# A two-layer adaLN program of eight batches: a weave with lags, the last batch in one weave, and the token shift's mix by scaled weights

## The chip, the cores and the metric

The kernel runs on one core of a Trainium2 chip. The core has five engines, each with its own instruction queue that is worked off in order: TensorE (PE, with its weight loads shown apart as PEld), VectorE (DVE), ScalarE (ACT), GpSimd (POOL) and SyncE (SP), which here only issues DMAs. The metric is the device time of one execution in microseconds. The kernel before takes 2069.03 us, the median of 3 runs (2065.26 to 2073.69).

## The reference

The input is x, 8 batches of 512 tokens of 128 channels. Two layers follow each other, and each has two halves of the form x + g * F(LN(x) * (1 + c) + s), with s, c and g from a modulation per batch.

```
h = LN(x)*(1+ca)+sa;  x = x + ga * L0_attn(h)        # layer 0, first half
h = LN(x)*(1+cb)+sb;  x = x + gb * L0_ffn(h)         # layer 0, second half
h = LN(x)*(1+ca)+sa;  x = x + ga * L1_attn(h)        # layer 1, first half
h = LN(x)*(1+cb)+sb;  x = x + gb * L1_ffn(h)         # layer 1, second half
```

- L0_attn: LN, then causal attention with 16 heads of 8 channels, and beside it a state-space branch (a causal convolution, a scan over time with 16 states for each of 256 channels, a gate, a product). The two are mixed, and an LN with a GELU FFN (512 hidden) follows.
- L0_ffn: a shared SiLU FFN and 8 experts of the same form, weighted by a router's top 2.
- L1_attn: attention over a band, with batch and sequence changed over, so that for each of 512 positions the 8 batches attend to each other.
- L1_ffn: a token shift. With x' the token before, xr = mu_r*x + (1-mu_r)*x' and xk = mu_k*x + (1-mu_k)*x'; the output is sigmoid(xr W_r) * (relu(xk W_k)^2 W_v).

## The kernel before, in words

**Tiling.** Activations lie channels by tokens, 128 x 512, one tile for a batch; all products are float32 apart from the causal mask, which is added by bfloat16 products with an identity. PSUM has eight banks: a ring of three (`mm_tile`, L148) for all products that leave at once, four for two score tiles of two banks each (`products`, L480), and one for the attention's sum.

**The parts of a batch's work**, all Python generators that issue a few instructions and then yield a cost:
- `head` (L816): load x, two layer norms. `normalised` (L237) is the norm: product with a centring matrix (`_m`), square and copy on ACT, a mean by small products (`_v`), + eps on DVE, the power -1/2 on POOL, a spread by four products (`_rb`), a product on DVE; `layernorm` adds ACT's scale and bias.
- `ssm_inputs` (L655): convolution, gate and steps, and `ssm_scan` (L741): for 16 units of two states, DVE's product hs (L783), two scans (L788), POOL's product of hs (L792), and `add`, a DVE sum of the two states (L764) and a POOL sum into xc (L765). B and C come from DRAM by broadcast loads (bc). `add` of a unit is issued behind the first scan of the next.
- `attention` (L438): four head groups g. `projections` (q, k), `maxima` (s, and DVE's maxima, L520), `shifts` (transposed maxima mT, and DVE's sum into qT, L539), `exponentials` (e, and ACT's exp, L558), `values` (av), `projected` (den, DVE's reciprocal rd, rb, DVE's product, and for each second group the product ao).
- `tail` (L826): LN and GELU FFN of L0_attn, the LN of L0_ffn, and `routing`: r, lg, top 2. `experts` (L934): for the shared FFN and 8 experts four products e (L945) with ACT's SiLU, four products e (L960), and DVE's weighting wb (L968) with a POOL sum moe (L971). `dispatch` writes the weights through DRAM: wT, a store wd, broadcast loads wb.
- `attention2` (L302): LN (lnc), products kv and q, then `attended`: POOL products pr (L358), DVE sums sc (L348), softmax, POOL products pv (L393), DVE sums ao (L387). Its result goes to DRAM (`kept`), apart from the last batch's.
- `mixing` (L1109): for one of eight slices of 448 tokens: load, transpose (aoT), residual xa, LN (lnd), `mixed_channels` (L1060): ACT scales the past token by 1-mu, DVE adds mu times the token (L1067), once for r and once for k; products ck, cr, cv; output transposed (oT) and stored. `closing` and `closed` do the remaining 512 + 512 tokens.

**The order.** PE, ACT and DVE run in the order in which these generators are advanced. `weave` (L200) takes parts with a cost in all and a begin and end, and always advances the part with the least progress. `paced` (L221) adds an order on DVE behind the latest marked softmax instruction. The loop L1004 runs a weave for each batch b: rest of attention(b), scan(b), head(b+1), attention2(b-2), ssm_inputs(b+1), the begin of attention(b+1), and `behind`, which is tail and experts of b-1. After the loop, the score banks are given back (L1025) for a ring of five (`l1_tile`), and a weave lays tail and experts of batch 7 beside attention2(6) and the mixing of slices 0 to 3; another lays attention2(7) beside slices 4 to 7 (L1232); closing follows.

Of the kernel before, what the change touches and what calls it, by code (L numbers as in the profile page):

```python
# [68 lines left out]
MSK, NMSK = _cols(_MASK)  # L69


@with_exitstack
def kernel(
# [126 lines left out]
    def weave(*parts):  # L200

        live = []
        for k, (pieces, whole, begin, end) in enumerate(parts):
            live.append([begin, k, iter(pieces), (end - begin) / whole])
        while live:
            part = min(live)
            cost = next(part[2], None)
            if cost is None:  # L210
                live.remove(part)
            else:
                part[0] += cost * part[3]
# [23 lines left out]
    def normalised(src, name, lane, cost=0.9, n=T, ring=mm_tile, wait=0.0):  # L237
# [5 lines left out]
        yield 0.2  # L243
# [4 lines left out]
        yield 2 * cost - 0.2  # L248
# [16 lines left out]
        yield cost + wait  # L265
# [11 lines left out]
        yield cost  # L277
        return d

    def layernorm(dst, src, scale, bias, name, lane, cost=0.9, n=T, ring=mm_tile, wait=0.0):  # L280
# [3 lines left out]
        yield cost  # L284
# [17 lines left out]
    def attention2(s, at):  # L302
# [6 lines left out]
        for i0 in range(0, NB, 2):  # L309
# [15 lines left out]
            yield 0.9  # L325
# [13 lines left out]
        yield 0.9  # L339
        yield from paced(attended(s, at, q, kv))  # L340

    def attended(s, at, q, kv):
# [13 lines left out]
        for i in range(NQ):  # L356
# [7 lines left out]
            yield 1.6  # L364
# [8 lines left out]
        yield 1.6  # L373
# [16 lines left out]
        for i in range(NQ):  # L390
# [10 lines left out]
            yield 1.6  # L401
# [20 lines left out]
    with ExitStack() as l0:  # L422
# [15 lines left out]
        def attention(b):  # L438
# [23 lines left out]
            def projections(g):  # L462
# [15 lines left out]
                yield 0.9  # L478
# [29 lines left out]
            def maxima(g, step):  # L508
# [19 lines left out]
                yield 0.6 + 0.25 * c0 / P  # L528

            def shifts(g):  # L530
# [10 lines left out]
                yield 1.2  # L541
# [3 lines left out]
            def exponentials(g, step):  # L545
# [15 lines left out]
                yield 0.6 + 0.25 * c0 / P  # L561
# [23 lines left out]
            def projected(g):  # L585
# [14 lines left out]
                yield 0.9  # L600
# [11 lines left out]
                yield 0.9  # L612
# [20 lines left out]

            yield from projections(0)
            for k in range(len(STEPS)):
                yield from maxima(0, k)
            for g in range(NG):
# [3 lines left out]
                )  # L641
                for k in range(len(STEPS)):
                    yield from exponentials(g, k)
                    next(others, None)
                    if g + 1 < NG and k:
                        alone(maxima(g + 1, k - 1))
                    values(g, k)
                    yield 0.85 + 0.25 * k
                    next(others, None)
                if g + 1 < NG:  # L650
                    yield from maxima(g + 1, len(STEPS) - 1)
                alone(others)
            yield from projected(NG - 1)

        def ssm_inputs(b, xn):  # L655
# [36 lines left out]
            yield 1.8  # L692
# [11 lines left out]
            yield 1.7  # L704
# [6 lines left out]
            for c in range(NDI):  # L711
# [15 lines left out]
                yield 0.9  # L727
# [5 lines left out]
                yield 0.9  # L733
            yield 0.9
# [6 lines left out]
        def ssm_scan(b, h, xc, zs, bc, dt, dtx):  # L741
# [27 lines left out]
            for u, (n0, c) in enumerate(units):  # L769
# [16 lines left out]
                yield 0.3  # L786
                for n in range(NN):
# [5 lines left out]
                    yield 0.3  # L793
                    if n == 0 and summed:
                        add(*summed.pop())
                        yield 0.15
                summed.append((n0, c, hs))
            add(*summed.pop())
            yield 0.15
            for c in range(NDI):  # L800
                nc.gpsimd.tensor_mul(xc[c], xc[c], zs[c])
                yield 0.5
            yield 0.5
# [9 lines left out]
            nc.vector.scalar_tensor_tensor(h, ps, beta, h, op0=ALU.mult, op1=ALU.add)  # L813
            yield 1.0

        def head(b):  # L816

            load_x(b)
            yield 0.5
# [6 lines left out]
        def tail(b, h):  # L826
# [5 lines left out]
            for m in range(NFF):  # L832
# [4 lines left out]
                t = wk.tile([P, T], F32, tag="hid", name=f"hid{b}_{m}", bufs=4)  # L837
                nc.scalar.activation(t, ps, AF.Gelu, bias=cv("ffn_b1", m))
                hid.append(t)
            yield 3.4  # L840
# [13 lines left out]
            yield 3.4  # L854
            hm = act.tile([P, T], F32, tag="hm", name=f"hm{b}")
# [5 lines left out]
        def routing(b, hm):  # L861
# [5 lines left out]
            yield 0.9  # L867
# [25 lines left out]
            yield 0.9  # L893
            yield 0.9
# [14 lines left out]
            for _ in range(4):  # L909
                yield 0.9  # L910
# [23 lines left out]
        def experts(b, hm, we):  # L934
            acc = wk.tile([P, T], F32, tag="moe", name=f"moe{b}", bufs=1)
            wd = None
            for e in range(NE + 1):
# [13 lines left out]
                yield 3.4  # L951
# [22 lines left out]
                yield 3.4  # L974
# [4 lines left out]
        ready, inputs, routed = {}, {}, {}  # L979
        nc.sync.dma_start(out=wb_sb, in_=wb)  # L980

        def finish(b, h):

            yield from tail(b, h)
            yield from experts(b, *routed.pop(b))

# [15 lines left out]
        with tc.manual_schedule(engines={mybir.EngineType.PE, mybir.EngineType.Activation, mybir.EngineType.DVE}):  # L1002
            behind = None
            for b in range(NB):  # L1004
# [3 lines left out]
                parts = [(ahead, 42.7, 0.0, 1.0)]  # L1008
                parts.append((paced(ssm_scan(b, h, *inputs.pop(b))), 19.3, 0.0, 0.83))
                if b + 1 < NB:  # L1010
                    parts.append((head(b + 1), 9.5, 0.1, 0.55))
                if b >= 2:
                    parts.append((attention2(b - 2, a2), 23.4, 0.0, 1.0))
                if b + 1 < NB:
                    parts.append((after(b + 1), 8.0, 0.8, 0.97))
                    ahead = attention(b + 1)
                    parts.append((some(ahead, BEGUN), 7.3, 0.85, 1.0))
                if behind:
                    parts.append((behind, 91.5, 0.0, 1.0))
# [5 lines left out]
            banks.close()  # L1025
            pl1 = l0.enter_context(tc.tile_pool(name="pl1", bufs=5, space=PSUM))

            def l1_tile(name):
                return pl1.tile([P, 512], F32, tag="mm", name=name)

            LAST = NB - 1
# [5 lines left out]
            def kept2(name):  # L1037

                t = wk.tile([P, 2, T], F32, tag="ex", name=name)
                return t.rearrange("p k t -> p (k t)").rearrange("p (i k u) -> p i k u", k=2, u=U)  # L1040

            now, past = kept2("now"), kept2("past")
            x7, x0 = (
                act.tile([P, T], F32, tag=f"xc{k}", name=f"xz{k}").rearrange(
                    "p (i u) -> p i u", u=U
                )
                for k in range(2)
            )
            nc.vector.memset(past[:, :, 1, 0:1], 0.0)
            gate = own[:, 10 + NG + NDI * DS :]  # L1050
            nc.vector.tensor_scalar(gate, mods[1][:, 5, :], 0.5, None, ALU.mult)
# [8 lines left out]
            def mixed_channels(name, n, cur, prev, t, r):  # L1060

                for k, mu in enumerate(("mu_r", "mu_k")):
# [315 lines left out]
```

## Time and profile before

The profiled execution took 2073.63 us; its span, from the first to the last instruction, is 2071.8 us with a mean granted TensorE clock of 0.87.

| engine | busy us | share | instructions |
|---|---|---|---|
| PE | 1653.0 | 80% | 8762 |
| PEld | 795.4 | 38% | 8762 |
| DVE | 1441.0 | 70% | 1648 |
| ACT | 985.2 | 48% | 1413 |
| POOL | 1045.2 | 50% | 539 |

| row | count | busy us | mean ns |
|---|---|---|---|
| DVE scan, L788 | 256 | 442.8 | 1732 |
| POOL product, L792 | 128 | 386.7 | 3021 |
| PE first product of the experts, L945 | 576 | 315.5 | 679 |
| DVE product before the scans, L783 | 128 | 249.5 | 1949 |
| POOL sum, L765 | 112 | 199.1 | 1778 |
| DVE maxima, L520 | 256 | 193.9 | 808 |

A float32 product stands in the trace as two matmuls. A row's idle time is that of its engine just before it, and the name behind the arrow is what ended most of it. A wait names the instruction that waited, the one that released it, the time in all, the number and the longest.

### The profile page before, as it was taken

To read this page: it belongs to the slowest core of one execution; us is meant where nothing else is said; L and a number is where in the kernel's file an instruction comes from. 1 tells how busy PE (TensorE), PEld (TensorE's weight loads), DVE (VectorE), ACT (ScalarE), POOL (GpSimd) and SP (SyncE) were. 2 spreads that over 40 slices of the span, in tenths; PEclk is the share of its full clock that TensorE was granted. 3 is DMA by queue.
4 is the path that set the end of the run, shared out by engine and by line. 5 is a ranking of instruction groups with operands and counts; after the bars stand their busy time and mean duration, and the time that the engine had idled before them with its cause. 6 is when DMAs were issued, how large, how long until landed. Compare 5 with 4: busy or idle time off the path is not lost. (4 is left out here: it accounts for less than half of the span.)

```text
span 2071.8 us, 22824 instructions
## 1 busy us (share of the span) xinstructions
PE 1653.0 (80%) x8762; PEld 795.4 (38%) x8762; DVE 1441.0 (70%) x1648; ACT 985.2 (48%) x1413; POOL 1045.2 (50%) x539
## 2 busy tenths in 40 slices
PE   5765888888798887888789788888788768868864
PEld 3332343434343443334334443334333333344442
DVE  1798688647894798668885889568876889352255
ACT  2532555464544644455445554464536454423432
POOL 1566355535673566444772667355763567331131
PEclk9766789998999988999889898999889989968975
DMA  3220123121222122121212122121312122102200
GB/s 101 78 71 21 53 70 99 52 83 56 82 71 78 46 77 82 46 79 59 94 56 83 54 73 78 47 82 60 98 47 78 57 87 81 50 9 76 71 8 18
DMA packets 67405, 135.32 MB, mean 65 GB/s; under 512 B 7864, under 2 KB 23360, under 8 KB 67168
## 3 DMA queue, kind: packets, MB, share of 16 engines
q1 hardware_dynamic: 66816, 131.51, 20.5%
q10 hardware_dynamic: 288, 1.93, 0.3%
q8 instruction: 69, 1.13, 0.2%
q0 software_dynamic: 192, 0.42, 0.1%
q14 instruction: 40, 0.33, 0.1%
HBM read 129.24 MB, written 4.59 MB: 65 GB/s over the span
## 5 line engine op out<-in xcount | busy, mean ns | idle before, releaser
L788 DVE TENSOR_TENSOR_SCAN hs<-da,hs 128x512 f32<-128x512 f32 x256 | 442.8, 1732 | 6.5 <-DVE hs L783 0.5
L792 POOL TENSOR_TENSOR hs<-hs,bc 128x1024 f32<-128x1024 f32 x128 | 386.7, 3021 | 102.2 <-DVE hs L788 83.9
L945 PE MATMUL e<-hm,we 128*128 128x512 f32 x576 | 315.5, 679 | 84.7 <-DVE wb L968 45.6
L558 ACT ACTIVATE ex<-e 128x768 f32<-128x768 f32 (+1 forms) x192 | 158.8, 879 | 317.4 <-PE e L496 317.0
L765 POOL TENSOR_TENSOR xc<-xc,hs 128x512 f32<-128x512 f32 x112 | 199.1, 1778 | 200.1 <-DVE hs L764 200.1
L960 PE MATMUL e<-eh,we 128*128 128x512 f32 x576 | 272.1, 616 | 0.3
L783 DVE TENSOR_TENSOR hs<-bc,dtw 128x1024 f32<-128x1024 f32 x128 | 249.5, 1949 | 0.0
L949 ACT ACTIVATE eh<-e,vec_sb 128x512 f32<-128x512 f32 x288 | 188.5, 686 | 122.1 <-PE e L945 115.2
L520 DVE TENSOR_REDUCE mpad<-s 128x2 f32<-128x256 f32 (+3 forms) x256 | 193.9, 808 | 39.4 <-PE s L496 39.4
L971 POOL TENSOR_TENSOR moe<-moe,wb 128x512 f32<-128x512 f32 x64 | 94.2, 1472 | 223.8 <-DVE wb L968 223.8
L945 PEld LDWEIGHTS e<-hm,we 128*128 128x128 f32 x576 | 111.6, 214 | 241.2 <-issue 89.3
L488 PE MATMUL e<-qT,kT 32*128 32x512 f32 (+3 forms) x1024 | 135.0, 580 | 81.7 <-DVE qT L539 75.3
L750 ACT ACTIVATE da<-dtu,own 128x512 f32<-128x512 f32 x256 | 169.8, 719 | 12.6 <-POOL dtu L737 12.2
L960 PEld LDWEIGHTS e<-eh,we 128*128 128x128 f32 x576 | 108.5, 198 | 127.3 <-issue 113.8
L968 DVE SCALAR_TENSOR_TENSOR wb<-e,vec_sb,wb 128x512 f32<-128x512 f32 x64 | 47.7, 745 | 150.5 <-DMA wb<-wd 58.4
L488 PE MATMUL s<-kT,qT 32*128 32x128 f32 (+3 forms) x1024 | 134.7, 524 | 10.4 <-DVE mpad L520 5.5
L764 DVE TENSOR_TENSOR hs<-hs 128x512 f32<-128x512 f32 x112 | 93.7, 837 | 37.9 <-POOL hs L792 37.9
L393 POOL TENSOR_TENSOR pv<-kv,sc 128x1024 f32<-128x1024 f32 x32 | 62.2, 1952 | 108.4 <-DVE ao L387 90.6
L496 PEld LDWEIGHTS <-ident_b 128*128 128x128 bf16 x1024 | 63.4, 103 | 138.0 <-issue 131.3
L358 POOL TENSOR_TENSOR pr<-kv,q 128x1024 f32<-128x1024 f32 x32 | 88.5, 2777 | 33.6 <-DVE sc L348 18.6
L488 PEld LDWEIGHTS e<-qT,kT 32*128 32x128 f32 x1024 | 51.2, 214 | 139.3 <-DVE qT L539 84.7
L572 PE MATMUL av<-ex,va 128*32 128x512 f32 (+3 forms) x1024 | 99.1, 478 | 0.0
(277 smaller groups left out, 2488.5 us busy)
## 6 DMA issues: line engine op xcount, KB each, us to landing
bc<-bc SPq DMA_DIRECT2D x128, 512.0 KB, 3.8
we<-in_w_dram SPq DMA_DIRECT2D x144, 256.0 KB, 3.1
wb<-wd SPq DMA_DIRECT2D x64, 256.0 KB, 3.3
xin<-in_x_dram SPq DMA_DIRECT2D x8, 256.0 KB, 2.9
wa_sb<-in_wa_dram ACTq DMA_DIRECT2D x1, 1832.0 KB
kept<-ao SPq DMA_DIRECT2D x14, 128.0 KB, 2.5
ai<-kept SPq DMA_DIRECT2D x56, 32.0 KB, 2.2
out_dram<-xout SPq DMA_DIRECT2D x16, 96.0 KB, 2.3
```

The costliest lines, as they stand in the source:

```text
L488: nc.tensor.matmul(tiles[i // 2][:, i % 2, c0 : c0 + n], lhsT=lhs[quadrant(i)], rhs=rhs[quadrant(i)], start=True, stop=False,)
L520: nc.vector.tensor_reduce(mpad[:, qi, 2 * pr : 2 * pr + 2, HD : HD + 1], tiles[pr][:, :, a : a + n], AX.X, ALU.max, negate=True,)
L558: nc.scalar.activation(t[:, :, :c0], tiles[pr][:, :, :c0], AF.Exp)
L572: nc.tensor.matmul(avs[g][quadrant(i), kj * P :], lhsT=va[:, kj, at : at + 32], rhs=ex[i // 2][:, i % 2, c0 : c0 + n], start=(kj == 0), st ...
L750: nc.scalar.activation(da[:, n, :], dt[c], AF.Exp, scale=A_sb[:, c, n0 + n : n0 + n + 1])
L765: nc.gpsimd.tensor_add(y, y, hs[:, 0, :])
L783: nc.vector.tensor_mul(hs, bcs[0], dtx[c].unsqueeze(1).to_broadcast([P, NN, T]))
L788: nc.vector.tensor_tensor_scan(hs[:, n, :], da[:, n, :], hs[:, n, :], 0.0, ALU.mult, ALU.add)
L792: nc.gpsimd.tensor_mul(hs, hs, bcs[1])
L945: nc.tensor.matmul(ps, lhsT=we1[:, m * P : (m + 1) * P], rhs=hm, start=True, stop=True)
L949: nc.scalar.activation(t, ps, AF.Silu, bias=cv("b1", e * NFF + m))
L960: nc.tensor.matmul(ps, lhsT=we2[:, m, :], rhs=hid[m], start=(m == 0), stop=(m == NFF - 1),)
```

## The change

**The weave.** A step may carry, beside its cost, a lag and the PE time that it stands for. `weave` counts the PE time issued so far (`now`). A part whose last step's results are due later than `now` is held back by 0.06 of progress for each unit that is missing. Nearly all steps get a lag and a PE time; those of the scan and of ACT's or DVE's own steps have a PE time of 0. The attention's products for the next group, which were issued without a yield of their own, are now steps too, and its whole cost is 64.3 where it was 42.7. In the scan, `add` is issued behind the second scan of the next unit.

```diff
+class Step(float):
+    def __new__(cls, cost, lag=0.0, pe=None):
+        self = super().__new__(cls, cost)
+        self.lag, self.pe = lag, cost if pe is None else pe
+        return self
+SOON = 0.06
...
-            live.append([begin, k, iter(pieces), (end - begin) / whole])
+            live.append([begin, k, iter(pieces), (end - begin) / whole, 0.0])
+        now = 0.0
         while live:
-            part = min(live)
+            part = min(live, key=lambda p: (p[0] + SOON * max(0.0, p[4] - now), p[1]))
             cost = next(part[2], None)
             if cost is None:
                 live.remove(part)
-            else:
-                part[0] += cost * part[3]
+                continue
+            part[0] += cost * part[3]
+            now += getattr(cost, "pe", cost)
+            part[4] = now + getattr(cost, "lag", 0.0)
...
-        yield cost + wait
+        yield Step(cost + wait, 5.0, 0.9)
...
-                yield 1.2
+                yield Step(1.2, 3.0, 0.5)
...
-                yield 0.3
+                yield Step(0.3, 0.0, 0.0)
                 for n in range(NN):
...
-                    yield 0.3
-                    if n == 0 and summed:
+                    yield Step(0.3, 0.0, 0.0)
+                    if n == NN - 1 and summed:
                         add(*summed.pop())
-                        yield 0.15
+                        yield Step(0.15, 0.0, 0.0)
```

**The last batch.** The loop runs over batches 0 to 6. One weave then holds attention, scan and attention2(5) of the last stage, the tail and experts of batch 6 and of batch 7, attention2(6) and the first four slices. `finish` waits, by steps of no PE time, until the attention and the scan of its batch have been issued whole, and its experts until those of the batch before have. `l1_tile` gives the score banks back at its first use. The last batch's hidden tiles and hm lie in other buffers, and each slice is a part of its own, whose norm buffers are passed on through `lanes`.

```diff
         def finish(b, h):
+            while b not in joined or joined[b] < 2:
+                yield Step(0.3, 1.0, 0.0)
             yield from tail(b, h)
+            while b and not done[b - 1]:
+                yield Step(0.3, 1.0, 0.0)
             yield from experts(b, *routed.pop(b))
+            done[b] = True
...
             weave(
-                (behind, 91.5, 0.0, 1.0),
-                (
-                    chain(through(LAST - 1), *(pair(i, (MIX, SECOND)) for i in range(0, SHARE, 2))),
-                    23.4 + 11.7 * SHARE, 0.0, 1.0,
+                (ahead, 64.3, 0.0, 0.86),
+                (paced(ssm_scan(LAST, h, *inputs.pop(LAST))), 19.3, 0.0, 0.74),
+                (attention2(LAST - 2, a2), 23.4, 0.03, 0.8),
+                (behind, 92.0, 0.0, 1.0),
+                (finish(LAST, h), 92.0, 0.87, 1.85),
+                (through(LAST - 1), 23.4, 1.02, 1.3),
+                *(
+                    (mixing(i, (MIX, SECOND)[i % 2]), 11.0, 1.33 + 0.13 * i, 1.6 + 0.13 * i)
+                    for i in range(SHARE)
                 ),
             )
```

**The mix.** Behind attention2(6), `begun` scales the weights W_r and W_k by mu and by 1-mu, four tiles of 128 x 128 on ACT. `mixed_channels` then adds two products in PSUM, of the token and of the past token, in place of the scaling on ACT and the sum on DVE.

```diff
+                kept2["w"] = act.tile([P, 4, C], F32, tag="at", name="wmix", bufs=3)
+                for k, name in enumerate(("r", "k")):
+                    for j, mu in enumerate((cv(f"mu_{name}"), omu[:, k : k + 1])):
+                        nc.scalar.activation(
+                            kept2["w"][:, 2 * k + j, :], cwb(name), AF.Identity, scale=mu
+                        )
...
-                for k, mu in enumerate(("mu_r", "mu_k")):
...
-                    nc.scalar.activation(tk, prev, AF.Identity, scale=omu[:, k : k + 1])
-                    nc.vector.scalar_tensor_tensor(
-                        tk, cur, cv(mu), tk, op0=ALU.mult, op1=ALU.add
-                    )
-                yield 0.9
+                def product(k, ps):
+                    for j, rhs in enumerate((cur, prev)):
+                        nc.tensor.matmul(
+                            ps, lhsT=kept2["w"][:, 2 * k + j, :], rhs=rhs,
+                            start=(j == 0), stop=(j == 1),
+                        )
```

## The prediction

> **What bounds the kernel now.** I read the page's busy shares first (PE 80%, DVE 70%, ACT 48%, POOL 50% of 2071.8 us), then cut the span into stages at the moments when TensorE transposes a batch's first score maxima (mT, group 0), then asked one steady stage for its waits. From 452.7 us on five stages last 228.0 to 228.9 us each, so one of them stands for all. Columns of the next fence: stretch, its length, busy time of PE, PEld, DVE, ACT, POOL, the granted clock, DMA share, GB/s.
>
> ```profile
> 63.40:240.20 176.80, 125.37 (x804) 60.69 (x805) 142.09 (x130) 60.91 (x90) 94.65 (x45) 0.71 0.16 50
> ...
> 909.20:1137.80 228.60, 192.96 (x1057) 90.40 (x1056) 172.34 (x192) 118.85 (x165) 128.78 (x66) 0.90 0.23 70
> ...
> 1595.20:1807.30 212.10, 165.78 (x941) 75.53 (x939) 159.47 (x168) 103.62 (x141) 124.03 (x59) 0.92 0.22 67
> 1807.30:1964.80 157.50, 126.59 (x400) 66.43 (x400) 57.98 (x101) 56.18 (x102) 33.82 (x23) 0.84 0.19 54
> 1964.80:2071.80 107.00, 59.76 (x233) 37.61 (x232) 57.91 (x76) 29.79 (x63) 25.22 (x15) 0.68 0.05 13
> ```
>
> PE has 193 us of work in a stage of 228.6 and idles 35. Where, the stage's waits say (time in all, times, longest):
>
> ```profile
> PE e L488 <- DVE qT L539: 9.6, 2, 6.9
> PE e L945 <- DVE wb L968: 6.1, 1, 6.1
> PE lna_rb L269 <- POOL lna_r L264: 4.6, 1, 4.6
> PE ln_rb L269 <- POOL ln_r L264: 4.1, 1, 4.1
> PE e L945 <- ACT eh L949: 3.9, 4, 2.1
> PE lnc_m L242 <- DVE xT L975: 3.4, 1, 3.4
> PE rb L604 <- DVE rd L599: 2.0, 1, 2.0
> ```
>
> Seven waits make 33.7 of the 35 us, and nearly all end with DVE, or with a POOL power that DVE feeds. But DVE is not a slow bystander: by the rows' durations it has 145 us of work from a stage's first mT to the end of its scan, where PE has 147. **In that stretch the two engines are equally loaded**, both queues are in order, and PE can run only a few tiles ahead (three banks in the shared ring). After it PE has 50 us with little for DVE.
>
> **Part 1, the order.** I take the order in which the changed program's instructions stand and give each the mean duration of its row. For each wait: PE work between producer and consumer, before and after. lnc_m behind xT: 2.5, then 6.7 us, so the 3.4 us go. e of group 2 behind its mT: 0, then 4.2, so 2.7 go. rb behind den of group 1: 2.6, then 10.5, so 2.0 go. e of group 3 waits 6.9 because qT's sum stands behind a DVE sum that waits 4.7 us for POOL's product; the change issues that sum one scan later, so I let 6.9 go. wb's 6.1 us is a round trip through DRAM behind one of the scan's loads in SP's queue; from wT to wb's place on DVE stood 6.9 us, now 10.3, so 6.1 go too. That is 21 us. lna_rb: 3.7, then 6.2. ln_rb (the L0 FFN's norm): 0, then 5.0. If those two also went, 30 us a stage would go.
>
> They do not, because of **what the order puts ahead of these instructions on DVE**. A scan piece now carries no PE time and no lag, so while the other parts are held back by their penalties, scan pieces are taken one after another. Stretches of DVE work that are scan alone: the longest was 9.5 us, now 13.0 and 12.0 in a steady stage; in the last batch 19.6, 14.6, 12.0 and 11.8 where it was 9.5. Walked through for a steady stage, with DVE's qT sum at 0:
> - ln_r stood 5.8 us after it, now 13.5; its power takes 1.6 and stands behind two products of 3.0 and one of 1.8 on POOL. PE reaches ln_rb 10.4 us on: it waits about 6 where lnc_m and ln_rb waited 7.5.
> - lna_rb waits about 3.5 (4.6).
> - lnb_d stands behind the run of 12.0 and starts near 66.7. Behind it are ACT's hm and PE's router product r, which PE reaches near 59: a new wait of 8, and 3 more for the next bank of the ring.
> - The second half has DVE 131 us on where PE is 118 on (wb of expert 4): about 6.5.
> - The eh waits of 3.9 stay.
>
> Sum 31 us where 34 were: 3 gained. A bound without any wait says the same from the other side: DVE's work up to the worst place plus PE's work behind it was 58 + 146 = 204 us, now 58 + 154 = 212.
>
> **The rule that speaks against longer scan runs.** The rows (min/median/max ns):
>
> ```profile
> L788 DVE TENSOR_TENSOR_SCAN hs<-da,hs x256: 1192/1218/3256, 76.4 to 1755.9; 128x512 f32<-128x512 f32 x128
> L783 DVE TENSOR_TENSOR hs<-bc,dtw x128: 1192/2218/3061, 74.7 to 1750.1; 128x1024 f32<-128x1024 f32 x128
> L792 POOL TENSOR_TENSOR hs<-hs,bc x128: 2336/3319/3351, 78.8 to 1759.5; 128x1024 f32<-128x1024 f32 x128
> ```
>
> The same instruction takes 1.2 or 3.2 us. The Trainium skill, "SBUF — State Buffer", section "Who interferes with whom", says that a DVE instruction with two SBUF inputs and a GpSimd instruction that reads SBUF exclude each other, whole instruction by whole instruction, while a DVE instruction with one SBUF input is free. By the rows' means a unit of two states costs DVE 1.95 + 2 x 1.73 + 0.84 = 6.25 us. By the rule, in a run with no other DVE work to lie beside POOL, it costs its own 1.2 + 2 x 1.2 + 0.67 = 4.3 plus POOL's 2.34 + 1.26 = 3.6: 7.9, a quarter more. The runs over 7 us hold 23 us more than before: by the row 0, by the rule up to 6 us a stage; I take 3, since half of each run meets a POOL product already now. New waits that I cannot place (the power behind POOL products, ACT's hm ahead of qT and kT in its queue): bounds 0 and 6.6 (two products of 3.3), I take 3. A steady stage then costs -3 + 3 + 3 = +3; stages 1 to 6: **+18** (bounds -60 and +48).
>
> Stage 0 (no experts; DVE 142 of 177): the bound goes from 118 + 34 = 152 to 106 + 54 = 160 us. I take **+6** (0 to +10).
>
> **Part 2, the last batch in one weave.** `finish` waits until attention and scan have both joined. In the order the last batch's FFN norm stands right behind its last attention product, as before, and 5 us of PE work before the end of batch 6's experts, where it stood 2 behind them (batches count from 0): **hardly anything is overlapped anew.** What does change is the scan: it is to be done by 0.74. Bound before: DVE 142 to the last mT, then PE 42: 184 (taken: 212). Now DVE 123 to expert 2 of batch 6, then PE 82: 205, because PE reaches so with 112 us done where it had 139. Of the +21 some falls into waits that were there; **+12** (0 to +25).
>
> The last batch's FFN and experts (157.5 us, PE work 130 in both orders): the mixing tiles come 25 us of PE work later, so the fetch wait (5.0), an eh wait behind the softmax (5.8) and one ck wait (2.9) go: **-12** with 1.7 kept back (-15 to 0).
>
> **Part 3, the mix by products.** It removes the 16 DVE sums of 1045 ns and 16 ACT scalings of 607, and those of the two closing tiles; PE gets a second ck and cr each: 8 x (1.22 + 1.03) + 2 x (1.45 + 1.09) = 23.1 us, by the rows of the first ones. Four small ACT scalings make the weights behind batch 6's second attention, in no one's way.
>
> ```profile
> L1067 DVE SCALAR_TENSOR_TENSOR mix<-xa,vec_sb,mix 128x384 f32<-128x384 f32 x16 | 16.0, 1045 | 10.0 <-ACT mix L1066 10.0
> ...
> L1072 PE MATMUL ck<-mix,wb_sb 128*128 128x384 f32 x16 | 10.5, 750 | 16.1 <-DVE mix L1067 16.1
> ```
>
> In the end stretch (107 us, PE 60) the waits of ck (13.3), ck_z (5.2), lnc_m (3.1) go, and half of an lnd_rb wait (6.3) that stood behind the mix. But PE's work behind the experts grows from 55 to 77 us by the order: 8 us of it stand before lnc_m and 9 more before the queries, so the last attention, a chain of POOL and DVE, starts that much later. +22 + 8 for that start's own exposed share - 25 = **+5** (-10 to +20).
>
> **Sum.** The profiled execution took 2073.63 us, 1.8 more than its span: 2073.6 + 18 + 6 + 12 - 12 + 5 = 2102.6. The three timed runs have their median 4.6 us below the profiled one, so I predict **2098 us**.
>
> **Rivals.**
> - *The scan runs decide* (the sum above), 0.48; own range 2080 to 2125.
> - *The lags win* (faster), 0.28. For it: the distances grow at all seven waits, and DVE has 56 us idle a stage to absorb the runs. It decides where ln_rb and r wait under 3 us each instead of 6 and 8: then a steady stage gains 6, six of them 36, and with +4, +8, -12, +5 the time is 2073.6 - 31 - 4.6 = 2038.
> - *A wash*, 0.12: waits change places at equal size, near 2070. The equal load of the two engines speaks for it.
> - *The port decides*, 0.12: every unit costs near 7.9 in the runs and DVE bounds each stage at +8 to +10: 56 + 10 + 20 + 0 over 2069 is 2155.
>
> What can be told from no change here is about 0.5%. Faster by more 0.28, within 0.12, slower 0.60. The range, 2030 to 2140, takes in the first three and the lower part of the last.
>
> **What would show it.** Right: steady stages near 232 us; a new PE wait at r behind hm or lnb_d of some 8 us; no lnc_m wait; scans with a mean above 1.73 us; the last batch's so with PE 112 us in; ck without a wait. Wrong: stages under 225 us, or ln_rb's wait under 3 us, which would mean that the penalties hide more than the runs cost.

## The result, and the profile after

The changed kernel takes 2247.61 us (median of 4 runs, 2241.94 to 2253.47) where the kernel before took 2068.03 beside it: a ratio of 1.0865, 95% interval 1.0826 to 1.0904. It is slower, as forecast, but by 180 us where the sum had 29; the forecast of 2098 and its range up to 2140 missed it. The profiled execution took 2253.47 us.

The table puts each stage of after beside the sum of the prediction (us). The stages begin where the prediction cut them; the last batch's ends where both its last attention product and batch 6's experts are through. In the kernel before these two ends lie 1.7 us apart, in after the experts end 5.5 us later, so part of what this stage loses and the next one gains is the place of the cut; their sum, +37.7, is not.

| stage | before | after | change | predicted |
|---|---|---|---|---|
| start | 63.4 | 64.0 | +0.6 | 0 |
| 0 | 176.8 | 202.4 | +25.6 | +6 |
| 1 | 212.5 | 243.8 | +31.3 | +3 |
| 2 to 6 (five) | 228.5 each | 241.8 to 246.9 | +83.6 in all | +15 |
| last batch's | 212.1 | 260.4 | +48.3 | +12 |
| its FFN and experts | 157.5 | 146.9 | -10.6 | -12 |
| end stretch | 107.0 | 108.0 | +1.0 | +5 |

The windows of after (columns as in the same view of before):

```profile
64.00:266.40 202.40, 122.14 (x805) 58.03 (x806) 147.64 (x131) 66.96 (x97) 92.78 (x48) 0.70 0.13 44
1002.20:1248.10 245.90, 193.27 (x1057) 88.64 (x1056) 166.08 (x193) 120.21 (x165) 121.88 (x65) 0.88 0.22 65
1736.40:1996.80 260.40, 184.98 (x946) 82.84 (x944) 169.39 (x170) 100.47 (x137) 112.31 (x53) 0.80 0.19 55
1996.80:2143.70 146.90, 122.48 (x396) 64.14 (x397) 45.43 (x87) 53.52 (x94) 34.35 (x23) 0.86 0.19 53
2143.70:2251.70 108.00, 71.72 (x275) 43.73 (x273) 50.81 (x69) 25.14 (x55) 24.87 (x15) 0.75 0.07 16
```

PE's work in the steady stage is what it was (193.27 against 192.96 us), DVE's is not more. So the 17 us more are idle time: 52.6 us of PE where it was 35.6. TensorE's waits in that stage of after (waiter, releaser: us in all, times, longest):

```profile
PE e L975 <- DVE wb L998: 11.5, 4, 3.6
PE r L895 <- ACT hm L299: 11.0, 1, 11.0
PE xT L435 <- DVE ln_r L279: 6.8, 1, 6.8
PE lna_rb L285 <- POOL lna_r L280: 6.4, 1, 6.4
PE e L975 <- ACT eh L979: 6.0, 4, 3.0
PE ln_m L258 <- DVE h L647: 2.8, 1, 2.8
PE e L975 <- DVE ln_d L292: 2.3, 1, 2.3
```

Gone are the waits of lnc_m (3.4), of e behind qT (9.6) and of rb (2.0), as the prediction had it, and r behind hm (the router's product behind ACT's norm) is there. Of the five waits that it placed, r is as long as it had it and the other four are longer: together 41.7 us. The 11.0 at r stand behind the second long run of scans: DVE's lnb_d starts at 1076.52 us, and from 1063.60 to there DVE did scan work alone.

What such a run does is seen best on DVE itself. This is the timeline of DVE from the start of the same stage (start, duration, instruction; in brackets the idle time before it and what ended it):

```profile
1006.48 1.22 DVE L808 TENSOR_TENSOR hs<-bc,dtw 128x1024 f32<-128x1024 f32 x1
1007.79 2.34 DVE L813 TENSOR_TENSOR_SCAN hs<-da,hs 128x512 f32<-128x512 f32 x2
1010.05 1.20 DVE L808 TENSOR_TENSOR hs<-bc,dtw 128x1024 f32<-128x1024 f32 x1
1011.35 4.30 DVE L813 TENSOR_TENSOR_SCAN hs<-da,hs 128x512 f32<-128x512 f32 x2
...
1016.22 3.35 DVE L808 TENSOR_TENSOR hs<-bc,dtw 128x1024 f32<-128x1024 f32 x1
1019.50 0.15 DVE L279 TENSOR_SCALAR ln_r<-ln_v 128x4 f32<-128x4 f32 x1
...
1027.33 0.69 DVE L292 TENSOR_TENSOR ln_d<-ln_d,ln_rb 128x512 f32<-128x512 f32 x1 [3.68 <-PE ln_rb L285]
...
1032.61 1.95 DVE L536 TENSOR_REDUCE mpad<-s 128x2 f32<-128x256 f32 x4 [3.93 <-PE s L512]
...
1043.50 0.75 DVE L881 SCALAR_TENSOR_TENSOR h<-f,vec_sb,h 128x512 f32<-128x512 f32 x1 [4.47 <-PE f L874]
```

From 1006.48 to 1019.50 DVE does scan work alone. ln_r stands behind it, and PE, which needs the ring slot that ln_r frees, idles 6.8 us (xT in the waits above). Then it is DVE's turn: it idles 3.7, 3.9 and 4.5 us for PE's products. **Each engine idles for the other in turn**, PE while the run lasts and DVE behind it. Over the stage, DVE's waits for PE's scores and at the product behind rb, before and then after:

```profile
DVE mpad L520 <- PE s L496: 3.0, 3, 1.6
DVE at L611 <- PE rb L604: 0.4, 1, 0.4
...
DVE mpad L536 <- PE s L512: 21.3, 8, 4.5
DVE at L627 <- PE rb L620: 11.8, 3, 9.0
```

That DVE's idle time behind a run makes PE's next waits longer is read from this order of events; no run separates it.

**A run of that length does not cost PE time by itself.** The kernel before has one of 12.1 us in its steady stages (first and last instruction, what stands behind it, and PE's only wait from 1033 to 1047):

```profile
1033.97 2.83 DVE L788 TENSOR_TENSOR_SCAN hs<-da,hs 128x512 f32<-128x512 f32 x1
...
1043.88 2.23 DVE L783 TENSOR_TENSOR hs<-bc,dtw 128x1024 f32<-128x1024 f32 x1
1046.03 1.21 DVE L348 TENSOR_REDUCE sc<-pr 128x64 f32<-128x1024 f32 x1
...
PE e L945 <- ACT eh L949: 0.4, 1, 0.4
```

PE does not wait for DVE at all there: sc is a sum of attention2 that it does not need then. Behind the two runs of after stand ln_r and lnb_d, which PE does need, and it idles 17.8 us there.

The rows of the scan's instructions (min/median/max ns), and the closing products of the mix:

```profile
L813 DVE TENSOR_TENSOR_SCAN hs<-da,hs x256: 1154/1217/3311, 77.0 to 1923.3; 128x512 f32<-128x512 f32 x128
L808 DVE TENSOR_TENSOR hs<-bc,dtw x128: 1197/1728/3383, 75.3 to 1904.3; 128x1024 f32<-128x1024 f32 x128
L817 POOL TENSOR_TENSOR hs<-hs,bc x128: 2338/2646/3271, 79.4 to 1926.3; 128x1024 f32<-128x1024 f32 x128
```

```profile
L1111 PE MATMUL ck<-xa,wmix 128*128 128x384 f32 x32 | 12.6, 519 | 0.0
```

The scans did not get longer: their mean is 1594 ns (1732 before). And ck has no idle time before it any more. In the last batch's stage these are the longest single waits of PE; each is longer than the longest of the same stage before (9.1, e behind wb):

```profile
PE kv L329 <- DVE kv L336: 13.7, 1, 13.7
PE e L975 <- DVE wb L998: 13.1, 1, 13.1
...
PE lnc_v L270 <- DVE ln_r L279: 9.3, 1, 9.3
```

### The profile page after: what moved, and what is told of

Same layout as the page of the kernel before. It is cut to its first block, busy times and chain, and to the rows that moved or that the text cites. A ratio compares the mean times of both kernels' runs of the same rounds, so it can differ in the third digit from the quotient of the medians.

```text
span 2251.7 us, 23034 instructions
## 1 busy us (share of the span) xinstructions
PE 1682.2 (75%) x8802; PEld 798.2 (35%) x8802; DVE 1409.0 (63%) x1628; ACT 989.2 (44%) x1405; POOL 991.1 (44%) x539
## 4 chain that ended last, share of the span: by engine, by line
PE 45%; DVE 38%; issue 5%; ACT 5%; POOL 3%; DMA 3%; SPq 0%; DVEq 0%; POOLq 0%; ACTq 0%
DVE hs L813 12%; DVE hs L808 10%; PE e L975 8%; PE e L990 7%; DVE mpad L536 5%; PE s L504 3%; PE av L588 3%; PE e L504 3%; DVE hs L789 3%; PE f L860 2%; DMA wb<-wd 1%; PE f L874 1%; PE e L512 1%; PE s L512 1%; ACT L979 1%
## 5 line engine op out<-in xcount | busy, mean ns | idle before, releaser
L817 POOL TENSOR_TENSOR hs<-hs,bc 128x1024 f32<-128x1024 f32 x128 | 335.2, 2619 | 423.4 <-DVE hs L813 282.0
L975 PE MATMUL e<-hm,we 128*128 128x512 f32 x576 | 328.4, 701 | 146.0 <-DVE wb L998 81.7
L813 DVE TENSOR_TENSOR_SCAN hs<-da,hs 128x512 f32<-128x512 f32 x256 | 401.3, 1594 | 9.4 <-DVE hs L808 0.5
L808 DVE TENSOR_TENSOR hs<-bc,dtw 128x1024 f32<-128x1024 f32 x128 | 284.5, 2223 | 0.0
L790 POOL TENSOR_TENSOR xc<-xc,hs 128x512 f32<-128x512 f32 x112 | 222.9, 1990 | 125.3 <-DVE hs L789 125.3
L1001 POOL TENSOR_TENSOR moe<-moe,wb 128x512 f32<-128x512 f32 x64 | 84.8, 1325 | 222.1 <-DVE wb L998 211.5
L504 PE MATMUL s<-kT,qT 32*128 32x128 f32 (+3 forms) x1024 | 138.3, 518 | 37.3 <-ACT ex L574 23.1
L504 PE MATMUL e<-qT,kT 32*128 32x512 f32 (+3 forms) x1024 | 120.1, 537 | 40.7 <-DVE qT L555 30.6
L588 PE MATMUL av<-ex,va 128*32 128x512 f32 (+3 forms) x1024 | 111.8, 521 | 2.0 <-ACT ex L574 2.0
```

Of the source, the lines that this page charges most:

```text
L504: nc.tensor.matmul(tiles[i // 2][:, i % 2, c0 : c0 + n], lhsT=lhs[quadrant(i)], rhs=rhs[quadrant(i)], start=True, stop=False,)
L588: nc.tensor.matmul(avs[g][quadrant(i), kj * P :], lhsT=va[:, kj, at : at + 32], rhs=ex[i // 2][:, i % 2, c0 : c0 + n], start=(kj == 0), st ...
L790: nc.gpsimd.tensor_add(y, y, hs[:, 0, :])
L808: nc.vector.tensor_mul(hs, bcs[0], dtx[c].unsqueeze(1).to_broadcast([P, NN, T]))
L813: nc.vector.tensor_tensor_scan(hs[:, n, :], da[:, n, :], hs[:, n, :], 0.0, ALU.mult, ALU.add)
L817: nc.gpsimd.tensor_mul(hs, hs, bcs[1])
```

## The experiments

In what follows, theory A is this: the runs of scan work on DVE make the loss, far more than they were given in the sum. The rivals blame other parts of the change: the finer attention steps and new sizes in the weave, the last batch's order, the mix. All stages in us; "steady" is stages 2 to 5. The prediction and the expectations give the lengths of runs by order, with the rows' means (9.5 for the kernel before). The second column has what the traces show in stage 4: runs of over 9 us in which DVE does nothing but scan work. In e1_soon0 and e15_soon0_a0 the "last" stage ends with batch 6's experts, 22 us behind the attention.

| kernel | scan runs over 9 us | stage 0 | 1 | steady | last | rest | end | median us | ratio to before |
|---|---|---|---|---|---|---|---|---|---|
| before | 12.1 | 176.8 | 212.5 | 228.0 to 228.9 | 212.1 | 157.5 | 107.0 | 2068.03 | 1 |
| after | 13.1, 13.0, 10.5 | 202.4 | 243.8 | 241.8 to 246.9 | 260.4 | 146.9 | 108.0 | 2247.61 | 1.0865 |
| e1_soon0 | 10.5 | 186.2 | 211.3 | 239 | 226.3 | 140.0 | 106.2 | 2130.35 | 1.0278 |
| e2_scanpe | 10.3, 9.8 | 194.3 | 224.5 | 225.1 to 228.8 | 223.6 | 143.0 | 108.0 | 2093.96 | 1.0105 |
| e3_mixonly | 12.1 | 174.8 | 208.0 | 228.0 to 229.2 | 212.8 | 149.9 | 99.0 | 2059.19 | 0.9936 |
| e4_addlate | 12.9 | 175.4 | 216.0 | 224.7 to 225.8 | 210.8 | 158.9 | 105.2 | 2056.85 | 0.993 |
| e5_lump2 | eight of 11.2 to 15.5 | 188.8 | 230.3 | 246.2 to 248.8 | 228.6 | 158.5 | 108.4 | 2211.56 | 1.068 |
| e6_scanpe10 | 10.5 | 189.0 | 216.0 | 225.7 to 231.8 | 215.6 | 147.2 | 108.0 | 2087.73 | 1.0065 |
| e7_scanpe06_83 | 11.1 | 190.0 | 217.9 | 228.7 to 235.2 | 208.6 | 139.1 | 107.4 | 2090.91 | 1.0099 |
| e8_mixadd | 12.9 | 175.3 | 212.9 | 224.3 to 225.6 | 213.1 | 150.0 | 98.8 | 2041.25 | 0.9859 |
| e9_fine | 10.2 | 178.2 | 215.1 | 221.7 to 226.2 | 207.5 | 157.9 | 106.9 | 2053.54 | 0.9915 |
| e10_coarselag | 10.0, 9.8, 9.4, 9.4 | 192.6 | 233.9 | 238.8 to 242.4 | 228.9 | 139.3 | 108.6 | 2172.2 | 1.0502 |
| e11_begin | 10.5 | 179.5 | 213.6 | 240.2 to 242.3 | 221.8 | 156.9 | 105.2 | 2152.36 | 1.0395 |
| e12_weights | 11.4 | 185.9 | 211.4 | 224.6 to 229.4 | 208.2 | 158.4 | 108.4 | 2065.81 | 0.9977 |
| e13_after_a0 | 13.1, 12.3, 9.5 | 204.8 | 245.7 | 245.9 to 249.2 | 257.4 | 146.7 | 108.0 | 2269.12 | 1.0962 |
| e14_scanpe_a0 | none (7.5) | 194.1 | 224.3 | 221.6 to 225.7 | 225.5 | 148.2 | 111.7 | 2088.15 | 1.0075 |
| e15_soon0_a0 | 11.4 | 186.4 | 215.1 | 228.5 to 228.8 | 230.8 | 142.6 | 106.3 | 2077.97 | 1.0024 |

### Taking the runs away in two ways

e1_soon0 is the changed kernel without the hold-back:

```diff
-SOON = 0.06
+SOON = 0.0
```

> The changed kernel with the hold-back factor at 0: steps keep their lags and costs, but the order is by progress alone; the finer attention steps, the last batch's single weave, the sum one scan later and the mix by products stay. Theory A (the runs of scan pieces, which only the hold-back makes, cost the 180 us): scan runs over 7 us nearly vanish in this order, steady stages return from 246 to 226 to 234 us, the total to 2060 to 2110. Theory B (the finer attention steps, the new weights of the parts or the later sum cost it): it stays above 2180.

2130.35 us, ratio 1.0278 (1.0261 to 1.0295). 117 us of the loss go with the hold-back, but the time lies between the ranges of the two theories: the steady stage stays at 239, 10 us above before, although its longest run (10.5 us) is shorter than that of the kernel before. Something else in the change costs time too.

e2_scanpe keeps the hold-back and lets the scan's own steps move the clock on, so that the other parts come due while scans are issued:

```diff
-                yield Step(0.3, 0.0, 0.0)
+                yield Step(0.3, 0.0, 0.3)
...
-                    yield Step(0.3, 0.0, 0.0)
+                    yield Step(0.3, 0.0, 0.3)
```

> The changed kernel, but a scan step counts 0.3 of PE time where it counted 0, so that the other parts' lags run out while scan pieces are issued; hold-back 0.06 stays. In its order the longest scan run of a steady stage is 9.4 us (13.0 and 12.0 in the changed kernel, 9.5 before) and that of the last batch 9.4 (19.6). Theory A (length of the scan runs): steady stages at 228 to 236, total 2080 to 2130. Theory C (holding the other parts back moves PE work away from where it was ready, whatever the scan does): steady stages stay above 240, total above 2180.

2093.96 us, ratio 1.0105 (1.0089 to 1.0122). **One number in two lines takes 154 of the 180 us away**; the steady stages fall from some 245 to 225, PE's waits in one of them to 34 us, DVE's wait for the scores from 21.3 to 13.9. In the last batch's stage the change is 37 us. The steady stages lie even a little under theory A's range. But the edit also lets the lags of all other parts run out sooner, so it does not single out the runs by itself.

### Making the runs in the kernel before

e5_lump2 is the kernel before, whose scan yields once for two units, so that some 12 us of it are issued together, eight times a stage:

```diff
+            owed = 0.0
...
-                yield 0.3
+                owed += 0.3
...
-                    yield 0.3
+                    owed += 0.3
...
-                        yield 0.15
+                        owed += 0.15
+                if u % 2:
+                    yield owed
+                    owed = 0.0
```

> The kernel before with nothing changed but that the scan yields once for two units (four states), so that DVE gets it in runs of 12 us, eight of them a stage; no lags, no new steps. Theory A (long scan runs alone cost what the changed kernel lost): stages of 240 to 255 us, total 2150 to 2280. Rival (runs cost only together with the lags' PE order): total under 2110.

2211.56 us, ratio 1.068 (1.0651 to 1.071), steady stages of 246 to 249. Nothing else of the change is in it. TensorE's longest waits in its stage from 981.7 us:

```profile
PE ln_rb L269 <- POOL ln_r L264: 10.8, 1, 10.8
PE rb L604 <- DVE rd L599: 9.2, 1, 9.2
PE q L465 <- DVE kv L320: 7.2, 1, 7.2
PE e L949 <- DVE at L611: 6.2, 1, 6.2
```

The three longest are for short instructions (ln_r, rd, kv) that stand directly behind a run. Seven of the eight runs last 11.2 to 12.3 us and the fifth 15.5, yet PE's longest wait at each is, in their order, 10.8, 1.1, 3.7, 7.2, 9.2, 5.1, 0.4 and 6.2 us. In six of them PE waits for the very instruction behind the run, or for what hangs on it (ln_r, mpad, kv, rd, wb, at); the other two have attention2's lnc_d and sc behind them, and cost 1.1 and 0.4. With e2_scanpe, theory A is shown from both sides, with this addition: **what stands behind a run sets its price**. By length alone e4_addlate below, with a run of 12.9 us and stages of 225, would contradict it.

### The mix and the late sum alone

e3_mixonly is the kernel before with the mix by products:

```diff
-                for k, mu in enumerate(("mu_r", "mu_k")):
...
-                nc.tensor.matmul(ps, lhsT=cwb("k"), rhs=t[1], start=True, stop=True)
+                product(1, ps)
...
-                nc.tensor.matmul(ps, lhsT=cwb("r"), rhs=t[0], start=True, stop=True)
+                product(0, ps)
```

> The kernel before with the mix by products alone. By the prediction's terms: PE gets 23 us more, of which 9 lie in the experts' stretch of the last batch, and the ck and ck_z waits (13.3 + 5.2 in the end stretch) go: 2060 to 2085, near 2070. Rival: PE has room there, so the end stretch shortens by the freed DVE time, 2050 or less.

2059.19 us, ratio 0.9936 (0.9919 to 0.9952): 7.6 us less in the experts' stretch and 8.0 in the end stretch, just under the first range.

e4_addlate is the kernel before with the sum of a unit behind the second scan of the next:

```diff
-                    if n == 0 and summed:
+                    if n == NN - 1 and summed:
```

> The kernel before with the scan's sum of two states issued one scan later and nothing else. If the sum's wait for POOL's product (4.7 us a stage) held up qT's sum and with it e of group 3 (6.9 us a stage): 5 to 7 us less in each of 7 stages, total 2020 to 2040. Rival: the later sum releases the scan's buffers later and lengthens the scan: 2070 to 2100.

2056.85 us, ratio 0.993 (0.9911 to 0.9948), 3.4 us less in a steady stage: half of what was expected, since the wait of e behind qT fell from 9.6 to 7.5 us and did not go. e8_mixadd has both:

> The kernel before with the mix by products and the scan's sum one scan later, both parts of the change that paid alone (13 and 16 us against the kernel before). They act in different stages (the end stretches; the eight scans), so they should add: 2039 to 2050, 1.0 to 1.6% under the kernel before. If both took the same slack: 2055.

2041.25 us, ratio 0.9859 (0.9834 to 0.9883). The two gains add, and this kernel beats both, by 1.4% and by 9%.

### Other settings of the counted scan

e6_scanpe10 counts 1.0 instead of 0.3 for a scan step; e7_scanpe06_83 counts 0.6 and lets the last batch's scan end at 0.83 instead of 0.74 (the edit of e7 against the changed kernel is shown):

```diff
-                yield Step(0.3, 0.0, 0.0)
+                yield Step(0.3, 0.0, 0.6)
...
-                (paced(ssm_scan(LAST, h, *inputs.pop(LAST))), 19.3, 0.0, 0.74),
+                (paced(ssm_scan(LAST, h, *inputs.pop(LAST))), 19.3, 0.0, 0.83),
```

> The changed kernel with a PE time of 1.0 for a scan step (0 in the changed one, 0.3 in the run before this). Longest run of a steady stage 7.7 us, none over 6 in the last batch. If shorter runs keep paying: steady stages 222 to 226, last batch's stage under 220, total 2060 to 2085. If the hold-back of 0.3 was already enough, 2085 to 2100; if counting scan time makes the lags run out too early, back toward the run without hold-back, 2110 to 2130.

> The changed kernel with 0.6 for a scan step, and the last batch's scan to be done by 0.83 of its weave where the change asks for 0.74. Against the run with 0.3: the last batch's stage falls from 224 to 212 to 216 (bound by DVE's work up to the worst place 192 us, it was 200), the rest is within 5 a stage: total 2065 to 2090.

e6: 1.0065 (1.0045 to 1.0085); e7: 1.0099 (1.007 to 1.0129). With the later end the last batch's stage falls to 208.6, below the kernel before and below what was expected; the steady stages of e7 give it back. e7 changes two numbers, so the later end's share is open: it is 15 us against e2_scanpe and 7 against e6. No setting tried brings the lags below the kernel before. One thing is worth noting: the last batch's stage and the experts' behind it take 347.7 us together in e7, where the mix alone has 362.7 (e3_mixonly). So the single weave for the last batch can gain time; a kernel with it and without the lags was not tried.

### What the rest is: one begin

e9_fine adds only the finer attention steps to e4_addlate, since they were suspected of the 239 us of e1_soon0:

```diff
-                    next(others, None)
+                    yield from one(others)
                     if g + 1 < NG and k:
-                        alone(maxima(g + 1, k - 1))
+                        yield from maxima(g + 1, k - 1)
...
-                parts = [(ahead, 42.7, 0.0, 1.0)]
+                parts = [(ahead, 64.3, 0.0, 1.0)]
```

> The kernel before with the sum behind the second scan, and the attention's products for the next group issued as steps of their own (whole cost 64.3 where it was 42.7); no lags, no other change. Without the lags the changed program's steady stage was 239 us, and with the late sum alone it is 225: what makes the 14 us between is open. Theory F (the finer steps make them, because the attention's products then come in the middle of other parts' work and DVE's maxima are asked for one by one): steady stages 235 to 241 us, the last batch's near 226, the time 2115 to 2145. Rival W (they come from the other weights and begins in the weave, which this kernel does not have): steady stages 224 to 228 us, the time 2050 to 2070.

2053.54 us, ratio 0.9915 (0.9891 to 0.9939). Theory F falls: the finer steps cost nothing. e10_coarselag is the reverse, e2_scanpe with the coarse steps:

```diff
-                    yield from one(others, 0.0 if follows else 2.4)
+                    did = float(next(others, 0.0))
...
-                        yield from maxima(g + 1, k - 1)
+                        did += sum(float(c) for c in maxima(g + 1, k - 1))
```

> The changed program with the scan's steps counted as 0.3 of PE time, and the attention's products for the next group issued without a step of their own, as before (whole cost 42.7; their PE time is counted in the step in front of them). Theory G (the lags' 14 us a steady stage are a gain of their own and add to the coarse steps): steady stages 210 to 217 us, the time 1985 to 2045. Rival M (the lags only mend what the finer steps cost): steady stages 223 to 229 us, the time 2070 to 2105.

2172.2 us, ratio 1.0502 (1.0479 to 1.0525): worse than either theory had it. Why the lags need the finer steps was not pursued. Its runs of over 9 us are no longer than those of e2_scanpe, four instead of two, and PE's longest wait at them is 5.1 us, so the runs alone do not explain it.

e11_begin and e12_weights put the other sizes of the changed weave on e9_fine, one number in the first, three places in the second:

```diff
-                    parts.append((attention2(b - 2, a2), 23.4, 0.0, 1.0))
+                    parts.append((attention2(b - 2, a2), 23.4, 0.03, 1.0))
```

```diff
-                    parts.append((after(b + 1), 8.0, 0.8, 0.97))
+                    parts.append((after(b + 1), 9.8, 0.8, 0.97))
...
-                    parts.append((behind, 91.5, 0.0, 1.0))
+                    parts.append((behind, 92.0, 0.0, 1.0))
...
-            yield 0.9
-            yield 0.9
+            yield 1.8
```

> The kernel before with late sum and finer attention steps, and attention2's part begun at 0.03 of the weave instead of 0.0, as in the changed program; its order on TensorE in a steady stage agrees with that of the changed program without lags to 96%. The finer steps alone left the steady stage at 225 us, so the 14 us of the changed program without lags are in what else it changes in the weave. Theory B (attention2's norm and products, begun later, meet DVE at the wrong place): steady stages 235 to 241 us, the time 2110 to 2145. Rival W (the other weights and the merged router steps): steady stages 222 to 228 us, the time 2045 to 2065.

> The kernel before with late sum and finer attention steps, and the changed program's other sizes in the weave: the whole cost of the next batch's inputs 9.8 where it was 8.0, that of tail and experts 92.0 where it was 91.5, the router's two steps of 0.9 made one of 1.8; attention2 begins at 0.0. Theory B (the later begin makes the 14 us): steady stages 222 to 228 us, the time 2045 to 2065. Rival W (these sizes make them): steady stages 235 to 241 us, the time 2110 to 2145. If neither this kernel nor its sister is slow, it takes both.

e11: 2152.36 us, ratio 1.0395 (1.0364 to 1.0425), a little over theory B's range. e12: 2065.81, 0.9977 (0.9964 to 0.9991). **The begin of attention2 at 0.03 instead of 0.0 costs 99 us by itself**, 17 a steady stage. On DVE, 11 of the 158 instructions from the stage's first scan product to the end of the scan change their place, ten of them attention2's (lnc_r, lnc_d, kv, q, sc), each a few instructions later. TensorE's longest waits in a steady stage of e11_begin:

```profile
PE e L488 <- DVE qT L539: 12.5, 3, 7.4
PE e L950 <- DVE wb L973: 8.9, 2, 4.5
PE e L950 <- DVE kv L320: 3.8, 1, 3.8
```

In e9_fine the same three are 6.3, 4.0 and 1.4 us. The waits are at the same places and at least twice as long. Which of the moved instructions starts them was not separated.

### How the two costs lie together

e13_after_a0, e14_scanpe_a0 and e15_soon0_a0 take the begin back to 0.0 (the diff of e11_begin reversed) in the changed kernel, in e2_scanpe and in e1_soon0.

> The changed program whole, with attention2's part begun at 0.0 of the weave, as before, instead of 0.03. Its scan runs become 13.0, 9.3 and 8.6 us where they were 13.0 and 12.0. Theory T (two costs side by side: the runs, and the later begin, 17 us a stage each without the other's help): steady stages 227 to 236 us, the time 2120 to 2180. Rival R (the runs alone decide in the changed program, the begin matters only where no lag holds it back): steady stages 240 to 247 us, the time 2215 to 2255. Rival N (the begin alone decides): 212 to 224, below 2100.

> The changed program with the scan's steps counted as 0.3 of PE time, and attention2 begun at 0.0. Theory T: the lags with counted scan already took the steady stage from 239 to 225, that is to where the kernel stands without the later begin, so they mend the begin and nothing else, and the earlier begin adds nothing: steady stages 222 to 228 us, the time 2080 to 2105. Rival L (the lags have a gain of their own): 209 to 217, the time 1995 to 2040.

> The changed program without lags (held back by 0), and attention2 begun at 0.0. Theory T (the begin alone makes the 14 us of the changed program without lags): steady stages 222 to 228 us, and with 226 for the last of them and 246 behind it a time of 2030 to 2060. Rival (the begin matters only in the order of the kernel before): steady stages 236 to 241, the time 2115 to 2140.

| steady stage us (median us) | begin 0.03 | begin 0.0 |
|---|---|---|
| before, late sum, finer steps | 240 to 242 (2152) | 222 to 226 (2054) |
| changed, no hold-back | 239 (2130) | 229 (2078) |
| changed, scan counted | 225 to 229 (2094) | 222 to 226 (2088) |
| changed | 242 to 247 (2248) | 246 to 249 (2269) |

e13: 1.0962 (1.0939 to 1.0984); e14: 1.0075 (1.0051 to 1.0099); e15: 1.0024 (1.0009 to 1.004). In the changed kernel the earlier begin gains nothing, and the time is even 1% longer, above rival R's range too: R's cause holds there, and theory T falls. T holds in the other two, though e15 is 18 us over its range. There the lags with a counted scan mostly mend what the later begin breaks (239 to some 226); on an order without that defect they gain 3 or 4 us (229 to 225), and end where the late sum alone had the steady stage.

## Why the prediction was wrong

**The step that failed is the size of what the scan runs cost in the steady stage**, "-3 + 3 + 3 = +3": the walk through the two queues (-3), the waits it could not place (+3), the lock (+3). The stage lost 17, all of it idle time of PE.

- The walk, -3, and the waits without a place, +3. It named the right places, and of its announced signs the wait at r (8, measured 11.0) and the end of lnc_m's, qT's and rb's waits came. But its sizes were short: ln_r's 6 became 6.8 (now at xT, which wants the ring slot), lna_rb's 3.5 became 6.4, r with the next bank 8 + 3 became 11.0, wb's 6.5 became 11.5, eh's 3.9 became 6.0, together 30.9 against 41.7; and another 11 us of small waits stood where it had 3 for them. The walk carried DVE's delay over to PE, and not PE's back to DVE. The timeline above has what it left out: 13 us of scan, then three waits for PE, 12 us of the next 24. It also took the runs' length for what was new, 13.0 and 12.0 us where 9.5 was; the trace of the kernel before has a run of 12.1. New is what stands behind the runs.
- The bound without waits. It rose by 8 us, from 204 to 212, and the stage by 17. It counts each engine's work and one change from DVE to PE; the stage before lay 24 us above it and that of after 34, and the trace shows waits in both directions in between.
- The lock, +3. From the rule of the Trainium skill, "SBUF — State Buffer", section "Who interferes with whom", the prediction worked out 7.9 us for a unit in a run. By the means of after's rows a unit costs DVE 2.22 + 2 x 1.59 + 0.83 = 6.24 us where it was 6.25, and in e5_lump2, which is nearly all runs, 1.76 + 2 x 1.82 + 0.78 = 6.17. The row was right and the sum drawn from the rule was not: this term is nothing. The announced mean of the scans, above 1.73 us, came as 1.59.

**Stage 0, +6.** It lost 25.6. e5_lump2 lost 12 there with runs alone, e1_soon0 9 without the hold-back, e2_scanpe 17 with the runs dissolved. The 9 are in the other sizes of the weave: e12_weights adds only these to e9_fine, and its stage 0 goes from 178.2 to 185.9. So of the 25.6, by these differences, some 8 or 9 are the sizes, 8 the lags, and 8 go when the scan is counted; the bound of 160 us saw none of them.

**The last batch's stage, +12.** It lost 48.3. e2_scanpe, with the runs dissolved, lost 11.5; the other 37 us go when the scan is counted, that is with the runs, which Part 1 had listed (19.6, 14.6, 12.0 and 11.8 us) and Part 2 gave nothing. The term for the scan's earlier end is of the right size in e2, but no run moves that end alone (e6 loses 3.5 with the same end), and its sign, PE 112 us in at so, came as 125 where it had been 135.

**Its FFN and experts, -12**: -10.6, and that was luck in part. The eh wait fell from 6.5 to 1.9 us and ck's 2.9 went, as forecast, but the fetch wait (aoT) grew from 5.0 to 13.3 instead of going; the mix alone gains 7.6 (e3_mixonly), and 5.5 us hang on the cut. **The end stretch, +5**: +1.0, within its range, but for the wrong reason: the mix by itself takes 8.0 us off it, and the rest of the change gives 9 back. The mix was a gain in both stretches. Its second products were given 23.1 us of PE; by after's rows all ck and cr products take 34.3 us where they took 25.9, so 8.4.

The late sum was priced only through qT's wait. By itself it is worth 3.4 us a steady stage.

**The rivals.** "The lags win" holds in no kernel run here: none with lags is faster than the kernel before. "The port decides" had the highest time, 2155, and named the stage's loss with the right sign and half its size, but for a cause that the rows refute. No rival had the begin of attention2; in the changed kernel it doesn't matter, but without the hold-back it decides between 239 and 229.

## What to carry to other kernels

Where two in-order engines carry the same load in a stretch, ask of each long run on one of them what stands directly behind it. A run of 12 us in front of a sum that nobody needed yet made TensorE wait for nothing here; two of 13 us in front of short instructions that TensorE needed made it idle 17.8 us in a stage that lost 17, and eight of 11 to 15 us, six of them in front of such instructions, made a stage of 228 us one of 246 to 249. When such an order is generated by priorities, make every step move the clock that priorities are measured in, else the work that counts for nothing is issued in one lump while all else is held back. And try each number of a schedule by itself: a part's begin moved by 3% cost 4.8% here, and a sum moved by one instruction gained 0.7%.

## What the hardware showed unexpectedly

The sum of DVE's time for a unit of the scan hardly depends on the order, though its parts do: with the late sum alone (e4_addlate) the scans fall from 1732 to 1518 ns, POOL's product from 3021 to 2540, while DVE's product rises from 1949 to 2168 and the sum from 837 to 1159; per unit DVE takes 6.36 us against 6.25, and POOL half a microsecond less. In e5_lump2 it is 6.17. So the time moves from one instruction to another, and long runs of scans did not make DVE's own work dearer.
